# Six early experts placed in a written order among the last two token tiles of the attention, their output over their own rows, their adds behind ranked gathers

## The chip, the core and the metric

The kernel runs on one core of one Trainium2 chip. The metric is the device time of one launch in microseconds (us); three runs of the kernel before gave 1723.81, 1723.93 and 1724.05 us, a median of 1723.93 us.

## What is computed

Four layers run one after the other on a 4 x 512 x 512 input, in float32. Only the last two matter for the change: a cross attention over 1024 context rows, and a mixture of 32 experts of which every token uses eight.

```python
# cross attention (last but one layer)
scores = einsum('bsd,bmd->bsm', hidden_states, memory_tokens) * scale   # masked
attn = softmax(scores, axis=-1)
out = einsum('bsm,bmd->bsd', attn, memory_tokens)
...
# mixture of experts (last layer): TOP_K = 8 of NUM_EXPERTS = 32
routing_weights, selected = top_k(softmax(x2d @ gate_kernel), TOP_K)
routing_weights /= sum(routing_weights)
sorted_inputs = take(x2d, argsort(selected) // TOP_K)
w0 = ragged_dot(sorted_inputs, gate_proj, group_sizes)    # 512 -> 192
w1 = ragged_dot(sorted_inputs, up_proj, group_sizes)      # 512 -> 192
expert_out = ragged_dot(silu(w0) * w1, down_proj, group_sizes)   # 192 -> 512
output = einsum('BKE,BK->BE', unsorted(expert_out), routing_weights)
...
x = x + _L1_xattn_ref(_layernorm(x), ctx_2048, mask)
x = x + _L1_ffn_ref(_layernorm(x), gate_kernel, gate_proj, up_proj, down_proj)
```

## The kernel before

The 2048 tokens stand in 16 tiles of 128 (0 to 15). The scores of the attention (L972) run from 725.5 us of the profile; the two layers before them are not touched.

**Attention.** A software pipeline runs over the tiles: at step t tile t is normalised (`norm_q`), tile t-1 gets its scores (`scores`), tile t-2 reads the context (`readout`), tile t-3 picks its eight experts (`choose`), and tile t-4 is entered into the lists (`place_rows`). `readout` transposes the probabilities, multiplies with the context (16 passes on PE, L999), adds to the residual, stores that to the output (L1007) and normalises the result into a row buffer `xr`. `choose` transposes `xr`, multiplies with the router (L1018), takes the top eight (`sel`), and stores the row with its weights to DRAM (`xn_d`, for tiles 0 to 10 also `xa_d`). `place_rows` makes positions with two tiny products on PE (L1049, L1050) and writes the token numbers into the lists `il_d` with eight indirect scatters on POOL (L1062) per tile.

**Early experts.** After tile 10 is placed, the first 256 list entries of experts 0 to 5 are final (`start_early`). Such an expert is worked on with two row tiles gathered from `xa_d` (`early_rows`: two indirect gathers on POOL, L899, into one of four big buffers) while the lists of the rest are still being written. Experts 4 and 5 use the buffers of 0 and 1 again.

**Ranked experts.** When all tiles are placed, `cnt` holds the count of every expert. VectorE ranks the experts by count (eight or so operations on 128 x 1024 elements, L1154 to L1163); rank r then gets the fixed shape `FIXED[r]` (the first is 7 tiles of 126 rows). The place of a ranked expert's list is read into a register on SP, the list is loaded (`load_list`, L911), which waits for all scatters, its rows are gathered on POOL (`load_rows`, L899, one gather per tile), its weights come over SP (`fetch`: three transfers, L891 to L893, 768, 256 and 128 KB, into one of three buffers).

**One expert.** Rows are transposed (`turn`, L1192, copied from PSUM by ACT and DVE in turn, L1184 and L1182), multiplied with gate and up (`gate_up`, L1211, three products, with silu on ACT, L1216 and L1221, and products on DVE, L1218 and L1226), multiplied with down (L1235, L1238), scaled by the routing weight (`finish`, ACT L1247 and DVE L1245) into one of three tiles `y`, and added to the output with one indirect accumulating transfer on POOL per row tile (`add_rows`, L1254). The adds of an expert wait until the adds of the expert before have landed. In the loop the transposes of the next part stand between `gate_up` and `down` of this one.

**What sets the order.** In this stage no order is written: a scheduler places the instructions of each engine by its own estimates, keeping dependencies. `tc.issue_after(ins)` keeps what is inside behind `ins` on its queue. Each engine and each queue runs in order. The early experts were six members of the list `work`, ahead of the ranked ones, all in one loop, and so their place among the last tiles of the attention was the scheduler's.

Of the kernel before, what the change touches and what calls it, by code (L numbers as in the profile page):

```python
# [18 lines left out]
P = 128  # L19
# [4 lines left out]
EARLY = 6  # L24
# [24 lines left out]
def kernel(  # L49
# [829 lines left out]
    xrs = [route_p.tile([P, XW], F32, name=f"xr{i}") for i in range(4)]  # L879
# [39 lines left out]
    scatters, begun = [], []  # L919
    with tc.tile_pool(name="ctx2", bufs=1) as ctx2, tc.tile_pool(  # L920
        name="aw", bufs=2
    ) as aw, tc.tile_pool(name="aps_s", bufs=2, space=PSUM) as aps_s, tc.tile_pool(
        name="aps_t", bufs=2, space=PSUM
    ) as aps_t, tc.tile_pool(name="aps_o", bufs=2, space=PSUM) as aps_o:
# [40 lines left out]
        def scores(t):  # L965
            b = t // TPB
            qt = aw.tile([P, DC, P], F32, tag="qt", name="qt")
            transpose_to(aps_t, xns.pop(t), qt)
            ps = aps_s.tile([P, M], F32, tag="sc", name="sc")
# [19 lines left out]
        def readout(t):  # L989
# [3 lines left out]
            for h in range(2):  # L993
                transpose_to(
                    aps_t, s[:, bass.ts(h, M // 2)], pt[:, bass.ts(h, MC // 2), :]
                )
            ps = aps_o.tile([P, 512], F32, tag="o", name="o")
            for c in range(MC):
                nc.tensor.matmul(  # L999
                    ps[:, :D], pt[:, c, :], values[b][c // (MC // 2)][:, c % (MC // 2), :],  # L1000
                    start=(c == 0), stop=(c == MC - 1),
                )
# [8 lines left out]
        def choose(t):  # L1011
# [3 lines left out]
            transpose_to(aps_t, xr[:, :D], rt)  # L1015
            ps = aps_o.tile([P, 512], F32, tag="o", name="o")
# [27 lines left out]
        def place_rows(t):  # L1044
# [3 lines left out]
            ps = aps_o.tile([P, 512], F32, tag="o", name="o")  # L1048
# [26 lines left out]
        def start_early():  # L1075

            nonlocal run
            ps = aps_o.tile([P, 512], F32, tag="o", name="o")
# [16 lines left out]
        def early_rows(e):  # L1095
            i = (2, 0, 1, 3)[e % 4]
            pool = big3 if i == 3 else big
            xg = pool.tile([P, ER, XW], F32, tag=f"big{i}", name=f"big{i}")
            for c in range(ER):
                gather(xg[:, c, :], xa_d, early[e][1][:, c : c + 1], CUT * P + P)  # L1100
            early_xg[e] = xg

        load_ctx(0)
        for step in range(NTT + 4):
            if step < NTT and step % TPB == 1 and step // TPB + 1 < B:
                load_ctx(step // TPB + 1)
            if step < NTT:
                norm_q(step)
            if 1 <= step < NTT + 1:
                scores(step - 1)  # L1110
            if 2 <= step < NTT + 2:
                readout(step - 2)
            if 3 <= step < NTT + 3:
                choose(step - 3)
# [4 lines left out]
            if step - 4 == CUT:  # L1119
                with tc.issue_after(scatters[-1]):  # L1120
                    for e in range(4):
                        early_rows(e)
        ps = aps_o.tile([P, 512], F32, tag="o", name="o")
        nc.tensor.matmul(ps[:, :E], ones, run, start=True, stop=True)
        nc.vector.tensor_sub(cnt, ps[:, :E], base1)
# [3 lines left out]
    M2 = MI - P  # L1129
    TM = max(t for t, _ in FIXED)  # L1130
    with tc.tile_pool(name="er", bufs=3, reuse_waits="tile") as er, tc.tile_pool(
        name="ei", bufs=2, reuse_waits="tile"
    ) as ei, tc.tile_pool(
        name="eps_g", bufs=2, space=PSUM, reuse_waits="tile"
    ) as eps_g, tc.tile_pool(
        name="eps_t", bufs=2, space=PSUM, reuse_waits="tile"
    ) as eps_t, tc.tile_pool(
        name="eps_d", bufs=4, space=PSUM, reuse_waits="tile"
    ) as eps_d, tc.tile_pool(name="rw", bufs=1, reuse_waits="tile") as rw:
# [9 lines left out]
        key = rw.tile([P, E], F32, name="key")  # L1149
# [3 lines left out]
        sq = rw.tile(square, F32, name="sq")  # L1153
        nc.vector.tensor_tensor(sq, inner(key), outer(key), ALU.is_gt)  # L1154
        rank = rw.tile([P, E], F32, name="rank")
# [4 lines left out]
        def by_rank(name, v, dtype=F32, scale=1.0, shift=0.0):  # L1160
            nc.vector.tensor_mul(sq, hot, inner(v))
            f = rw.tile([P, E], F32, name=f"{name}_f")
# [17 lines left out]
        def copy(i, dst, ps):  # L1180
            if i % 2:
                nc.vector.tensor_copy(dst, ps)  # L1182
            else:
                nc.scalar.copy(dst, ps)  # L1184

        def turn(xg, t0, nt, q):

            xgt = ei.tile([P, DC, 512], F32, tag="xgt", name="xgt")
            for c in range(DC):
                ps = eps_t.tile([P, 512], F32, tag="tr", name="tr")  # L1190
# [9 lines left out]
        def gate_up(gu, xgt, nt, q):  # L1200


            n = nt * q
            h1 = ei.tile([P, 512], F32, tag="h1", name="h1")
            h2 = ei.tile([P, 512], F32, tag="h2", name="h2")
            sg = ei.tile([P, 512], F32, tag="sg", name="sg")
            ps = []
            for k in range(3):
                p = eps_g.tile([P, 512], F32, tag="g", name="g")
# [5 lines left out]
                if k == 0:  # L1215
                    nc.scalar.activation(sg[:, :n], p[:, :n], AF.Silu)  # L1216
                elif k == 1:
                    mul = nc.vector.tensor_mul(h1[:, :n], p[:, :n], sg[:, :n]).ins  # L1218
                else:
                    s2 = ei.tile([P, 512], F32, tag="s2", name="s2")  # L1220
                    nc.scalar.activation(s2[M2:, :n], p[:M2, :n], AF.Silu)  # L1221
                    for o in range(min(2, nt)):
                        def odd(v):
                            return v.rearrange("p (t q) -> p t q", q=q)[:, o::2, :]
                        half = LOW if o else UP
                        nc.vector.tensor_mul(  # L1226
# [342 lines left out]
```

## Time and profile before

| what | value |
|---|---|
| three runs | 1723.81, 1723.93, 1724.05 us |
| the profiled execution itself | 1739.66 us |
| its span, first to last instruction | 1737.9 us |
| mean clock granted to TensorE | 0.983 |
| PE, DVE, ACT, POOL busy | 95%, 44%, 29%, 34% of the span |
| last scores of the attention end | 989.5 us |
| first product of a ranked expert (128 x 378) | 1114.13 us |

Line numbers (L1211) are those of the kernel before. PE is the matmul engine and PEld its weight load, DVE VectorE, ACT ScalarE, POOL GpSimd, SPq the queue on which most transfers are issued. A float32 matmul shows as two instructions (two passes). "issue" as a reason for idle time means that the profile shows nothing that the engine waited for.

### The profile page before, as it was taken

What the parts mean: (1) busy time and instruction counts of PE and PEld (TensorE: products, weight loads), DVE (VectorE), ACT (ScalarE), POOL (GpSimd) and SP (SyncE); (2) the same over time, 40 slices, a digit from 0 to 9 for tenths busy, and PEclk for the clock granted to TensorE, in tenths of its full rate; (3) what the DMA queues carried; (4) which work ended last, traced back from release to release, by engine and by line L of the source; (5) the groups of instructions that cost most, each with busy time, mean ns of one, the idle gap of its engine ahead of it and who ended that gap; (6) DMA issues with size and microseconds to landing.
All of it is one profiled execution on the core that took longest, in us unless ns stands there. A gap on an engine that the chain in (4) does not pass through costs nothing.

```text
span 1737.9 us, 17749 instructions
## 1 busy us (share of the span) xinstructions
PE 1659.3 (95%) x6050; PEld 1010.7 (58%) x6050; DVE 763.0 (44%) x1715; ACT 506.9 (29%) x852; POOL 596.4 (34%) x522
## 2 busy tenths in 40 slices
PE   7998999999999999999999968899999999999996
PEld 2685657776777776545555445455555666544443
DVE  4683457755775554434444334222222223232322
ACT  2510333322331111146656431122222222222221
POOL 1000130101010100104434467555565666456654
PEclk9999999999999999999999979999999999999998
DMA  9313110000000000454331128867777887668774
GB/s 346 122 50 120 49 64 26 1 1 0 1 1 25 0 1 1 157 181 100 92 93 52 30 79 174 205 135 157 159 153 156 205 184 160 148 167 188 180 158 64
DMA packets 92717, 181.76 MB, mean 105 GB/s; under 512 B 23905, under 2 KB 24545, under 8 KB 92624
## 3 DMA queue, kind: packets, MB, share of 16 engines
q0 software_dynamic: 40560, 73.04, 22.4%
q1 hardware_dynamic: 51198, 106.72, 19.7%
q8 instruction: 48, 0.79, 0.2%
q10 hardware_dynamic: 866, 0.85, 0.2%
q14 instruction: 45, 0.37, 0.1%
HBM read 132.38 MB, written 51.62 MB: 106 GB/s over the span
## 4 chain that ended last, share of the span: by engine, by line
PE 82%; DMA 5%; issue 5%; DVE 4%; POOL 2%; ACT 2%; another core or an unknown queue 1%; ACTq 0%; POOLq 0%; DVEq 0%; SPq 0%
PE g L1211 18%; PE q L717 17%; PE dn L364 11%; PE dn L1235 6%; PE o L999 5%; PE sc L972 5%; PE gu L342 5%; PE dn L1238 4%; PE tr L1192 3%; DMA out_dram<-y,ids 2%; PE tr L167 1%; DMA x_sb<-in_cn_dram 1%; PE o L1018 1%; DMA big<-xa_d,near 1%; POOL out_dram L1254 1%
## 5 line engine op out<-in xcount | busy, mean ns | idle before, releaser
L1211 PE MATMUL g<-xgt,gu 128*128 128x256 f32 (+25 forms) x1248 | 384.2, 464 | 3.4 <-ACT sg L1216 2.0
L1211 PEld LDWEIGHTS g<-xgt,gu 128*128 128x128 f32 x1248 | 234.3, 192 | 164.5 <-issue 81.7
L1254 POOL DMA_INDIRECT out_dram<-y,ids x153 | 242.8, 1587 | 131.2 <-ACT y L1247 45.6
L899 POOL DMA_INDIRECT xg<-xn_d,ids x141 | 151.0, 1071 | 143.9 <-issue 125.9
L364 PE MATMUL dn<-wdn,h 128*128 128x512 f32 x448 | 200.3, 593 | 0.0
L1062 POOL DMA_INDIRECT il_d<-tok,slots x128 | 127.0, 992 | 193.2 <-DVE sel L1032 85.8
L717 PE MATMUL q<-big,s 128*128 128x256 f32 x768 | 173.6, 379 | 0.0
L717 PEld LDWEIGHTS q<-big,s 128*128 128x128 f32 x768 | 145.9, 190 | 19.8
L1235 PE MATMUL dn<-d,h 128*126 128x512 f32 (+8 forms) x306 | 150.4, 598 | 0.4 <-issue 0.4
L364 PEld LDWEIGHTS dn<-wdn,h 128*128 128x128 f32 x448 | 84.1, 190 | 92.8 <-issue 91.6
L717 PE MATMUL q<-big,wgu 128*128 128x256 f32 x576 | 132.4, 379 | 0.0
L1218 DVE TENSOR_TENSOR h<-g,sg 128x256 f32<-128x256 f32 (+25 forms) x52 | 27.0, 520 | 232.1 <-PE g L1211 197.3
L717 PEld LDWEIGHTS q<-big,wgu 128*128 128x128 f32 x576 | 109.3, 190 | 25.7 <-issue 9.3
L342 PE MATMUL gu<-big,wgu 128*128 128x256 f32 x512 | 116.5, 384 | 3.3 <-ACT sg L349 3.3
L999 PE MATMUL o<-big,pt 128*128 128x512 f32 x256 | 115.2, 602 | 4.1 <-issue 3.5
L972 PE MATMUL sc<-big,qt 128*128 128x512 f32 x256 | 114.4, 600 | 0.3 <-ACT qt L170 0.3
L342 PEld LDWEIGHTS gu<-big,wgu 128*128 128x128 f32 x512 | 97.7, 192 | 26.4 <-issue 8.5
L374 POOL TENSOR_TENSOR x_sb<-x_sb,y 128x512 f32<-128x512 f32 x16 | 19.8, 1270 | 258.3 <-DVE y L373 258.3
L278 POOL TENSOR_TENSOR x_sb<-x_sb,beta_t 128x512 f32<-128x512 f32 x16 | 23.7, 1509 | 235.2 <-ACT y L267 222.8
L1247 ACT ACTIVATE y<-dn,w 126x512 f32<-126x512 f32 (+8 forms) x82 | 56.3, 687 | 139.6 <-PE dn L1238 137.1
L731 ACT ACTIVATE sg<-q,wsu_t 128x256 f32<-128x256 f32 x96 | 45.4, 473 | 171.5 <-DVE q L753 84.0
L1192 PEld LDWEIGHTS tr<-ident,xg 126*128 126x128 f32 (+8 forms) x564 | 64.4, 141 | 53.1 <-ACT xgt L1184 20.2
(233 smaller groups left out, 1883.2 us busy)
## 6 DMA issues: line engine op xcount, KB each, us to landing
gu<-in_w_gu_dram SPq DMA_DIRECT2D x38, 768.0 KB
big<-in_cn_dram SPq DMA_DIRECT2D x10, 1024.0 KB
d<-in_w_dn_dram SPq DMA_DIRECT2D x38, 256.0 KB
big<-in_ct_dram SPq DMA_DIRECT2D x8, 1024.0 KB
x_sb<-in_cn_dram SPq DMA_DIRECT2D x12, 512.0 KB
d<-in_w_dn_dram SPq DMA_DIRECT2D x38, 128.0 KB
xn_d<-xr SPq DMA_DIRECT2D x16, 272.0 KB
x_sb<-in_x_dram SPq DMA_DIRECT2D x4, 1024.0 KB
```

The lines of the kernel that those rows point to most:

```text
L342: nc.tensor.matmul(ps[:, :n], wt[:, c, fs], xhs[b][:, c, cols], start=(c == 0), stop=(c == DC - 1),)
L364: nc.tensor.matmul(ps[:, :D], h[:, i * P : (i + 1) * P], wdn[:, fc, :], start=(fc == 0), stop=(fc == FC - 1),)
L717: nc.tensor.matmul(q[:, m * HS : (m + 1) * HS], w[:, m, k, :], x[:, k, :], start=(k == 0), stop=(k == 1),)
L899: ins = nc.gpsimd.indirect_dma_start(out=xg, out_offset=None, in_=src[:, :], in_offset=bass.IndirectOffsetOnAxis(ap=idx, axis=0), bounds_c ...
L972: nc.tensor.matmul(ps[:, bass.ts(h, M // 2)], qt[:, c, :], keys[b][h][:, c, :], start=(c == 0), stop=(c == DC - 1),)
L999: nc.tensor.matmul(ps[:, :D], pt[:, c, :], values[b][c // (MC // 2)][:, c % (MC // 2), :], start=(c == 0), stop=(c == MC - 1),)
L1062: ins = nc.gpsimd.indirect_dma_start(out=il_d[:, :], out_offset=bass.IndirectOffsetOnAxis(ap=slots[:, j : j + 1], axis=0), in_=tok[:, t : ...
L1192: nc.tensor.transpose(ps[:, h * q : (h + 1) * q], xg[:q, t0 + h, c * P : (c + 1) * P], ident[:q, :q],)
L1211: nc.tensor.matmul(p[:, :n], gu[:, c, k * P : (k + 1) * P], xgt[:, c, :n], start=(c == 0), stop=(c == DC - 1),)
L1235: nc.tensor.matmul(p[:q, :D], h1[:, bass.ts(i, q)], d1, start=True, stop=False)
L1238: nc.tensor.matmul(p[:q, :D], h2[half, bass.ts(i, q)], d2[half, :], start=False, stop=True)
L1254: ins = nc.gpsimd.indirect_dma_start(out=of[:, :], out_offset=bass.IndirectOffsetOnAxis(ap=idx, axis=0), in_=y, in_offset=None, bounds_che ...
```

## The change

The early experts leave the list `work` and its class `Early` goes. They get three functions: `T(e)` transposes in four steps (a generator), `G(e, fill)` is gate and up, taking one step of `fill` behind every third matmul, `D_(e)` is down, scaling, and the fetch of the weights of expert e+3. The result of `D_` is written over the gathered rows themselves. `readout` and `choose` become generators that stop once after their transposes; `readout` can take a step of `T` ahead of every second matmul. The order on PE, DVE and ACT from tile 14's readout to the last early expert is then the written one (`manual_schedule`); POOL and SP keep theirs.

```diff
-        def readout(t):
+        def readout(t, among=lambda: None):
...
+            yield
...
             for c in range(MC):
+                if c % 2:
+                    among()
...
         def early_rows(e):
-            i = (2, 0, 1, 3)[e % 4]
-            pool = big3 if i == 3 else big
-            xg = pool.tile([P, ER, XW], F32, tag=f"big{i}", name=f"big{i}")
+            if e < 4:
+                i = (2, 0, 1, 3)[e]
+                pool = big3 if i == 3 else big
+                xg = pool.tile([P, ER, XW], F32, tag=f"big{i}", name=f"big{i}")
+            else:
+                xg = ee.tile([P, ER, XW], F32, tag="xg", name="xg")
...
-                    for e in range(4):
+                    for e in range(3):
                         early_rows(e)
+        wts = {e: fetch(e) for e in range(3)}
...
+        def T(e):
+            xgt = xgts[e] = ee.tile([P, DC, ER * P], F32, tag="xgt", name="xgt")
+            for c in range(DC):
+                ps = ps_t.tile([P, 512], F32, tag="tr", name="tr")
+                for h in range(ER):
+                    nc.tensor.transpose(
+                        ps[:, h * P : (h + 1) * P],
+                        early_xg[e][:, h, c * P : (c + 1) * P], ident,
+                    )
+                copy(c, xgt[:, c, :], ps[:, : ER * P])
+                yield
+        def G(e, fill=iter(())):
...
+                for c in range(DC):
+                    nc.tensor.matmul(
+                        p[:, : ER * P], wts[e][0][:, c, k * P : (k + 1) * P], xgt[:, c, :],
+                        start=(c == 0), stop=(c == DC - 1),
+                    )
+                    if (k * DC + c) % 3 == 2:
+                        next(fill, None)
...
+        def D_(e):
+            xg = early_xg[e]
+            _, d1, d2 = wts.pop(e)
+            for i, p in enumerate(down(*hs.pop(e), ER, P, d1, d2)):
+                finish(i, p[:, :D], xg[:, i, :D], xg[:, i, D + e : D + e + 1])
+            if e + 3 < EARLY:
+                wts[e + 3] = fetch(e + 3)
+        last = NTT - 1
+        scores(last)
...
+        with tc.manual_schedule(engines=order):
+            turned = T(0)
+            r14, c13 = readout(last - 1, lambda: next(turned, None)), choose(last - 2)
+            next(r14)
+            next(c13)
+            whole(r14)
+            whole(c13)
+            place_rows(last - 3)
+            with tc.issue_after(scatters[-1]):
+                early_rows(3)
+            turned = T(1)
+            r15, c14 = readout(last, lambda: next(turned, None)), choose(last - 1)
+            next(r15)
+            next(c14)
+            whole(c14)
+            whole(r15)
+            place_rows(last - 2)
+            with tc.issue_after(scatters[-1]):
+                early_rows(4)
+            G(0)
+            c15 = choose(last)
+            next(c15)
+            D_(0)
+            whole(c15)
+            place_rows(last - 1)
+            with tc.issue_after(scatters[-1]):
+                early_rows(5)
+            turned = T(2)
+            G(1, turned)
+            place_rows(last)
...
+        with tc.manual_schedule(engines=order):
+            early_adds(0, scatters[-1])
+            for k in range(3):
+                work[k].load_list()
+            turned = T(3)
+            G(2, turned)
+            D_(1)
+            for k in range(3):
+                work[k].load_rows()
+                if k == 0:
+                    early_adds(1, gathers[-1])
+            for k in range(3, LISTS):
+                work[k].load_list()
+            turned = T(4)
+            G(3, turned)
+            D_(2)
+            work[0].load_weights()
+            early_adds(2, gathers[-1])
+            turned = T(5)
+            G(4, turned)
+            D_(3)
+            work[1].load_weights()
+            early_adds(3, gathers[-1])
+            G(5)
+            D_(4)
+            early_adds(4, gathers[-1])
...
+        xgt = turned(*parts[0])
+        D_(5)
+        early_p.close()
+        early_adds(5, gathers[-1])
```

Smaller parts: the scratch of the ranking lies in the row buffers `xr`, now one tile; the 32 one-column fills of `most` move from the end of the expert stage to its preparation; PSUM pools of the attention (`ps_t`, `ps_o`) live on into the expert stage, `ps_g` and `ps_d` take the banks of the scores, and the down products rotate over two banks of `ps_d` and two of `ps_o` instead of four of one pool. The ranked loop itself is the old one, without the early experts.

## The prediction

> **What bounds the kernel now.** I first read the page's busy shares and the row of granted clock: PE is busy 95% of the span, and its clock is below full in one stretch. I then cut the span into windows to find it.
>
> ```profile
> PE 1659.3 (95%) x6050; PEld 1010.7 (58%) x6050; DVE 763.0 (44%) x1715; ACT 506.9 (29%) x852; POOL 596.4 (34%) x522
> 985.00:998.00 13.00, 12.71 (x39) 6.09 (x38) 3.17 (x6) 2.74 (x5) 9.96 (x11) 1.00 0.27 27
> 998.00:1014.00 16.00, 8.73 (x31) 5.86 (x30) 3.62 (x19) 5.63 (x8) 7.78 (x8) 0.68 0.50 170
> 1014.00:1030.00 16.00, 11.13 (x49) 8.12 (x48) 4.70 (x31) 5.63 (x9) 10.07 (x11) 0.76 0.12 35
> 1030.00:1064.00 34.00, 27.31 (x87) 16.43 (x87) 18.86 (x39) 5.35 (x11) 26.09 (x55) 0.81 0.42 47
> 1064.00:1085.00 21.00, 19.75 (x87) 13.45 (x86) 6.82 (x15) 5.07 (x11) 13.60 (x12) 1.00 1.03 281
> 1085.00:1114.00 29.00, 21.42 (x81) 12.66 (x79) 5.57 (x13) 3.90 (x9) 19.05 (x17) 0.89 1.01 275
> 1114.00:1174.00 60.00, 59.69 (x203) 31.13 (x202) 17.02 (x32) 13.78 (x25) 30.73 (x23) 1.00 0.64 122
> ```
>
> A window's columns are: stretch, length, busy time of PE, PEld, DVE, ACT and POOL, granted clock, DMA share, GB/s. From 985 to 1114 us, the end of the attention and the six early experts, PE is busy 101 of 129 us: 28 us idle. The clock takes more: 0.68, 0.76, 0.81 and 0.89 mean that about 37 us ran at half; some 5 of them were idle, so 32 us of work took twice its time: 16 us. Idle and clock make 44 us. From the other side: attention's rest (scores 4.5, two readouts 14.3, transposes, routers and placements about 12, from their rows) and six experts at 9.34 us (G to G, 1063.99 to 1073.33), 56, need about 87 us of 129. So 41 to 44 us is the most that any order can return. After 1114 PE is full to 1720 us, and nothing there is touched.
>
> The chain of waits names what halted PE:
>
> ```profile
> 993.85 6.43 DMA big<-xa_d,near
> 1001.63 4.84 issue
> 1010.15 4.50 PE o L999 x8
> 1023.37 1.13 PE tr L167 x4
> 1025.21 1.92 PE o L1018 x8
> 1040.66 3.95 another core or an unknown queue x2
> 1053.17 4.33 another core or an unknown queue
> 1081.26 9.43 DMA big<-xa_d,near
> ```
>
> Gathered rows that land late (6.43 and 9.43 us after issue); the last tile's normalisation, for which nothing else was placed (PE empty 1020.2 to 1023.4); and halts with no visible releaser (at 1001.6, 1042, 1056, 1091 and 1105.6 us: 4.8, 3.5, 2, 1.1 and 2.9 us, together 14). Behind three halts the clock is at half: 1002 to 1012, 1023 to 1036.5, 1108 to 1114 us.
>
> **The change, step by step.** I follow PE through the built program's order, with durations from the rows, in the profile's own microseconds. Tile 15's scores and eight transposes end as before at 990.6.
>
> 1. Readout 14. The first of its eight matmul pairs ends at 991.5. The next instructions are now T(0)'s two transposes of expert 0's gathered rows. Those gathers stay on POOL behind the scatters of tile 11, so they still issue from 993.85; in the trace the transposes that wait for them ran at 1000.65 and 1001.30. Before, PE did the readout meanwhile; now all of it waits behind T(0): 9.8 us lost, to 1001.3.
>
> ```profile
> 993.85 1.05 POOL L899 DMA_INDIRECT big<-xa_d,near  x1 [0.30 <-issue]
> 1000.65 0.30 PE L1192 MATMUL tr<-ident,big 128*128 128x128 f32 x1 [2.07 <-DMA big<-xa_d,near]
> 1001.30 0.33 PE L1192 MATMUL tr<-ident,big 128*128 128x128 f32 x1 [0.35 <-issue]
> ```
>
> Then 14/16 of 7.13 and T(0)'s 4 x 0.44: 8.0. The clock has gone. After the idle stretch from 1001.6 to 1006.5 the row shows half speed until 1012, 5.5 us of work, so I add 2.75: end 1012.1. The Trainium skill ("TensorE: Matmul & The Clock Gate", "What's actually happening") says that the clock halves after about 3.4 us of idleness and returns after about 3.4 us of sustained work, which speaks against a stall in mid-readout. By that rule the addition would be an estimated 1.7 us instead of 2.75, and the forecast 1 us lower.
>
> 2. Router 13 (1.08), placing tile 12 (0.8), transposes of tile 15's probabilities (1.06): 1015.0. Transposing tile 14's row needs its normalisation. Behind readout 15 that took 3.8 us without the exp between (add 1018.78 to about 1022.5), so 1015.9: wait 0.9. Router 14 needs ACT to load exp (1.28), do one exp (0.32), two copies of tile 15's probabilities (1.07) and the row's copy (0.58): 1019.2, wait 2.7. Two waits with almost no matmul between them: I add 2 for the clock. Router 1.08, readout 15 with T(1) 8.9: 1032. Placing tile 13 included.
>
> 3. G(0) 5.45 and the row transposes 0.6 cover the 3.8 us of normalisation 15 that left PE empty before; D(0) 2.8 covers the copy for router 15 (1.08); placing 14 0.8: 1042.8. G(1) with T(2) 7.2, placing 15 and the count 1.2: 1051.2. G(2) began at 1063.99 before.
>
> 4. Left until the first ranked product: four rounds of 9.34, one D more (2.8), 0.9 for the larger transposes: 41.1. That makes 1092.3. DVE's ranking (operations of 1.2 us) now stands between early copies: 1 us.
>
> The rows of rank 0 decide whether that holds. Placing tile 12 is queued on DVE behind weights that wait for ACT's exp 13, after tile 14's normalisation: its scatters start at 1019, not 1010.28. POOL needs 10.2 us per tile (8 x 1.275) and 2.6 for two gathers, now three times between the scatters: tile 15's end at 1070.8, where before they ended at 1055.8. Landing 4.5 and list 2.0 ("974.00 4.51 DMA il_d<-tok,slots" and the list behind it) overlap the adds of expert 0 (2 x 1.9): rank 0's gathers from 1077.5, the third issued by 1081.6. With 6.43 to 9.43 us to land that is 1088 to 1091, and T(rank 0) is due at about 1087. I take 2 us of wait: first ranked product at 1095.3.
>
> ```profile
> 1081.26 1.08 POOL L899 DMA_INDIRECT big<-xa_d,near  x1 [0.30 <-issue]
> 1090.82 0.30 PE L1192 MATMUL tr<-ident,big 128*128 128x128 f32 x1 [1.42 <-DMA big<-xa_d,near]
> 1116.03 1.54 POOL L1254 DMA_INDIRECT out_dram<-y,ids  x1 [7.10 <-DMA out_dram<-y,ids]
> 1132.19 1.62 POOL L1254 DMA_INDIRECT out_dram<-y,ids  x1 [2.06 <-DMA out_dram<-y,ids]
> ```
>
> 5. The halts without a releaser: bounds 0 and 23 us (14 and the half clock behind them, 9). Three of the five stand beside a DMA share near 1, where the new order still works; but the order gives PE more to do between waits. I take 5, one such halt: 1100.3 against 1114.1, a gain of 14.
>
> 6. Edits at nothing: the fills of `most` (1.1 us of POOL) stand early, under the feed forward's matmuls; scratch in `xr` moves nothing; the PSUM banks for down stay four; weights 0 to 2 were already fetched long before. Weights 3 to 5 issue as buffers come free. On SP expert 5's down weights and rank 0's weights queue behind the five lists, so they issue near 1077, and are due at 1088 and 1095: 10 us of cover, and at some 280 GB/s (row 1064 to 1085) 1.5 MB takes 5.4 us.
>
> The sum: -14 on this execution's 1739.66 gives 1725.7. It lies 15.7 us above the median, and I can't see where. Spread evenly, a gain of 0.8% makes 1723.93 into **1710 us**.
>
> **Rivals.** *Adds back up (slower).* Adds of experts 2 to 5 stand on POOL behind rank 2's gathers with no gather between them, so each waits until the last has landed. Gathers of ranks 0 to 2 are 19 x 1.37 and the adds of expert 1 3.9: adds 2 start at 1107.4. With landings of 4.7 (the row at 1132.19: the add before ended at 1127.45) and 3.9 per pair, rank 3's two gathers (2.7) and one more landing, rank 0's adds begin at 1141.7, and the first of the three `y` tiles is free at about 1152. PE needs it for the fourth part at 1100.3 + 57.7 = 1158. With landings as slow as the gather's 9.43, five times 4.7 us more, it is free at 1175.5: PE stalls 17.5, a loss of 3.5 after the gain: 1739.66 + 3.5, in the median 1727. It decides from landings of about 6 us and loses from about 9. For it: 7.10 in the row at 1116.03. Against it: DMA share falls to 0.64 after 1114. With every halt of point 5 back the result is similar: 1095.3 + 23 is 1118, 1728. Together 0.24.
>
> *The halts are the profile's own (no change).* If the 15.7 us between profile and median lie in this stretch, the unprofiled kernel loses only about 28 there, and the new order's own waits (9.8 + 2.75 + 3.6 + 2 + 3) take 21 of a possible 28 at most: gain 3 to 7, some 1721. For it: halts of this kind stand nowhere else in the trace. Chance 0.14.
>
> *A better order than I think.* No halts, rows on time: 1092, a gain of 22: 1702. Chance 0.15. That the order is not the written one is excluded by the built program: PE shows it.
>
> **Numbers.** Forecast (1705 to 1720) 0.47, better 0.15, no change 0.14, slower 0.24. The likeliest is 1710. The range 1698 to 1728 takes in both bounds of point 5 and the adds. About 0.2% (3.4 us) is what a measurement can tell from no change: faster 0.62, same 0.14, slower 0.24.
>
> **What would show it.** PE idle some 9 us at 991.5 in readout 14, with T(0) waiting for the DMA, and a half clock behind it; no gap between readout 15 and router 15; last scatter near 1071; first 128 x 378 product near 1095 to 1100; a wait for `y` in rank 1's second part only if adds back up. I am wrong if the gather lands before 991, if the halts all return, or if the first ranked product gains and the end does not.

## The result, and the profile after

The changed kernel is slower, by a third of a percent: 1730.16 us (1728.25 to 1732.34, 7 runs) beside 1723.93 us (1722.21 to 1727.35, 7 runs) for the kernel before; ratio 1.0033, 95% interval 1.0021 to 1.0045. The forecast was 1710.

The two profiled executions say the opposite: 1739.66 us before, 1730.79 after, 8.9 us less. The profiled execution after is one of its own timed runs; the one before is none of its own, and stood 15.7 us above their median. The same 8.9 us stand at the first ranked product, 1114.13 before and 1105.19 after; from there to the end both take 623.8 us. So what differs lies ahead of that product, nearly all of it behind 985 us. The windows of the changed kernel over the stretches that were shown for the kernel before (same columns):

```profile
985.00:998.00 13.00, 8.83 (x26) 3.89 (x24) 3.37 (x8) 3.67 (x7) 9.86 (x10) 0.89 0.29 27
998.00:1014.00 16.00, 12.10 (x42) 6.79 (x42) 2.51 (x6) 2.32 (x4) 2.99 (x3) 0.70 0.32 112
1014.00:1030.00 16.00, 12.19 (x39) 6.67 (x38) 4.71 (x28) 6.32 (x10) 8.88 (x9) 0.79 0.12 40
1030.00:1064.00 34.00, 32.84 (x162) 24.76 (x161) 22.63 (x59) 12.14 (x22) 21.25 (x20) 1.00 0.90 137
1064.00:1085.00 21.00, 18.20 (x69) 11.96 (x68) 7.95 (x22) 3.64 (x8) 12.03 (x11) 0.92 0.62 61
1085.00:1114.00 29.00, 19.70 (x68) 11.18 (x68) 5.96 (x13) 4.05 (x8) 19.48 (x18) 0.82 0.93 262
```

PE is busy for 104 of the 129 us, against 101 before. The idle time has moved: the middle (1030 to 1064) is nearly full and at full clock now, where it was 27 of 34 us at 0.81; the ends carry the idleness. The waits of PE in this stretch (total, number, longest) name all 25 us of it, and none is without a releaser (an event in the profile that ended the wait):

```profile
PE tr L1350 <- DMA xg<-xn_d,ids: 9.3, 3, 4.4
PE tr L1208 <- DMA big<-xa_d,near: 7.7, 2, 7.5
PE tr L167 <- ACT pt L170: 3.4, 2, 3.1
PE tr L1208 <- DMA xg<-xa_d,near: 2.8, 2, 1.6
PE g L1228 <- ACT sg L1171: 1.2, 1, 1.2
PE o L1038 <- ACT rt L170: 0.7, 1, 0.7
```

Line numbers in a run's rows are those of its own kernel; here L1350 are the transposes of ranked rows, L1208 those of early rows. So 9.3 us go to rank 0's rows, 7.7 to expert 0's in the middle of readout 14. The timeline of PE, POOL and SP's queue shows both, and the links between them:

```profile
1001.64 0.45 PE L1208 MATMUL tr<-ident,big 128*128 128x128 f32 x1 [7.52 <-DMA big<-xa_d,near]
1018.43 1.01 POOL L1082 DMA_INDIRECT il_d<-tok,slots  x1 [16.68 <-DVE slots L1079]
1074.65 0.97 POOL L1082 DMA_INDIRECT il_d<-tok,slots  x1 [0.30 <-issue]
1081.83 4.30 SPq L916 DMA_DIRECT2D ids<-il_d  x5
1086.32 1.13 POOL L904 DMA_INDIRECT xg<-xn_d,ids  x1 [6.92 <-DMA ids<-il_d]
1091.31 0.33 PE L1350 MATMUL tr<-ident,xg 126*128 126x126 f32 x1 [2.05 <-DMA xg<-xn_d,ids]
1096.03 0.47 PE L1350 MATMUL tr<-ident,xg 126*128 126x126 f32 x1 [4.39 <-DMA xg<-xn_d,ids]
1105.19 7.89 PE L1369 MATMUL g<-xgt,gu 128*128 128x378 f32 x24
```

Read from the bottom up: the first ranked product at 1105.19 waits for rows that POOL gathers from 1086.32; the gather waits for a list, loaded from 1081.83; the lists wait until the last scatter, issued at 1074.65, has landed; and the first scatter of tile 12 could not start before 1018.43, because POOL waited 16.7 us for its slots. From the last scatter to the first ranked product it is 30.5 us.

### The profile page after: what moved, and what is told of

Its sections match the earlier page's. It is cut to its first block, busy times and chain, and to the rows that moved or that the text cites. A ratio compares the mean times of both kernels' runs of the same rounds, so it can differ in the third digit from the quotient of the medians.

```text
span 1729.0 us, 17724 instructions
## 1 busy us (share of the span) xinstructions
PE 1653.6 (96%) x6050; PEld 1008.9 (58%) x6050; DVE 764.8 (44%) x1715; ACT 508.5 (29%) x853; POOL 596.8 (35%) x522
## 4 chain that ended last, share of the span: by engine, by line
PE 82%; DMA 6%; DVE 5%; ACT 3%; issue 2%; POOL 1%; SPq 0%; ACTq 0%; POOLq 0%; DVEq 0%
PE g L1369 19%; PE q L717 17%; PE dn L364 11%; PE o L1018 6%; PE dn L1186 6%; PE sc L988 5%; PE gu L342 5%; PE dn L1189 4%; DMA il_d<-tok,slots 2%; PE tr L1350 2%; DMA out_dram<-y,ids 2%; PE tr L167 1%; DMA x_sb<-in_cn_dram 1%; DVE h L1179 1%; PE o L1038 1%
## 5 line engine op out<-in xcount | busy, mean ns | idle before, releaser
L1369 PE MATMUL g<-xgt,gu 128*128 128x360 f32 (+24 forms) x1104 | 346.0, 470 | 0.0
L1369 PEld LDWEIGHTS g<-xgt,gu 128*128 128x128 f32 x1104 | 205.0, 190 | 149.9 <-issue 76.7
L1383 POOL DMA_INDIRECT out_dram<-y,ids x141 | 224.5, 1592 | 110.9 <-ACT y L1198 34.4
L1018 PE MATMUL o<-big,pt 128*128 128x512 f32 x256 | 119.4, 615 | 3.8 <-ACT pt L170 3.8
L1350 PEld LDWEIGHTS tr<-ident,xg 126*128 126x128 f32 (+8 forms) x564 | 65.0, 142 | 60.3 <-ACT xgt L1164 20.3
```

What stands on the lines that cost most here:

```text
L1018: nc.tensor.matmul(ps[:, :D], pt[:, c, :], values[b][c // (MC // 2)][:, c % (MC // 2), :], start=(c == 0), stop=(c == MC - 1),)
L1350: nc.tensor.transpose(ps[:, h * q : (h + 1) * q], xg[:q, t0 + h, c * P : (c + 1) * P], ident[:q, :q],)
L1369: nc.tensor.matmul(p[:, :n], gu[:, c, k * P : (k + 1) * P], xgt[:, c, :n], start=(c == 0), stop=(c == DC - 1),)
L1383: ins = nc.gpsimd.indirect_dma_start(out=of[:, :], out_offset=bass.IndirectOffsetOnAxis(ap=idx, axis=0), in_=y, in_offset=None, bounds_che ...
```

## The experiments

Each set below ran on one chip with the kernel before beside it as a yardstick (time: median, lowest and highest of its runs). The sets differ in that yardstick, which turned out to be the main finding. The record names the chips of sets 1 to 6 as 1, 5, 3, 2, 15 and 2; sets 4 and 6 have the same number and 13 us between them.

| set | kernel before, us | what ran |
|---|---|---|
| first measurement | 1723.93 (1722.21 to 1727.35) | changed 1730.16 |
| 1 | 1751.01 (1737.04 to 1757.57) | b_again, t0_in_r15, place_early, both |
| 2 | 1747.91 (1732.18 to 1755.60) | after_again, t0_again, a_plain, a_nowts |
| 3 | 1750.90 (1736.85 to 1757.29) | b_plain, six_first, t0_six, after_third |
| 4 | 1734.77 (1730.32 to 1745.06) | b_side, t0_one, b_third |
| 5 | 1724.25 (1721.69 to 1728.40) | after_fourth, six_again |
| 6 | 1747.44 (1736.40 to 1756.58) | t0_six_again |

### Set 1: undo T(0) in readout 14, place tiles earlier

`b_again` is the kernel before, unchanged.

> The kernel before, unchanged, profiled a second time. Theory H (the five halts without a releaser belong to that one profiled execution and not to the timed runs): this profile shows none or other ones, and its first ranked product (128 x 378) comes near 1098 us instead of 1114.13, its span near 1722. Rival (the halts are in every run of the kernel): the same halts near 1002, 1042, 1056 and 1106 us, first ranked product near 1114, while the time stays near 1724 and the 15.7 us lie elsewhere.

`t0_in_r15` moves expert 0's transposes one readout later:

```diff
-            turned = T(0)
-            r14, c13 = readout(last - 1, lambda: next(turned, None)), choose(last - 2)
+            r14, c13 = readout(last - 1), choose(last - 2)
...
-            turned = T(1)
+            turned = T(0)
...
-            G(0)
+            G(0, T(1))
```

> The changed kernel with one edit: T(0) is taken among readout 15 instead of readout 14, T(1) inside G(0). Theory A (the wait for expert 0's rows inside readout 14, 1001.6 us, holds up PE and, through tile 12 to 15's placing, the rows of rank 0): readout 14 ends near 1000, everything behind it some 11 to 13 us earlier, first ranked product near 1093 instead of 1105.2, time near 1717. Theory B (rank 0's rows are late for reasons behind that: scatters that wait for landings and lists, whatever PE does): first ranked product no earlier than 1102, time 1727 or more.

`place_early` moves `place_rows(last - 3)`, with the early rows behind it, ahead of readout 14, and the later tiles' placements forward likewise; `both` is the two edits together.

> The changed kernel with one edit: each tile is placed as soon as its choice is known (12 ahead of readout 14, 13 ahead of router 14, 14 behind readout 15, 15 at the first step among G(1)), with the gathers of experts 3 to 5 behind them; T(0) stays in readout 14. Theory B (the row chain sets the first ranked product): last scatter issued near 1055 instead of 1075.6, rank 0's rows there before PE wants them, first ranked product at PE's own 1095, time near 1720. Theory A (only PE's wait in readout 14 counts): within 2 us of 1730.

> Both edits together. A and B both: PE's own path is 11 to 13 us shorter and the rows come in time: first ranked product near 1084, time near 1709. If the adds of experts 2 to 5 then back up on POOL (three tiles y full in the fourth part), PE waits for y near 1140 to 1150 and the time stays at 1714 or above.

Measured: b_again 1744.26; t0_in_r15 1727.31 (ratio to the kernel before 0.9886, 0.9842 to 0.9930); place_early 1741.11 (0.9967, 0.9937 to 0.9997); both 1745.63 (0.9986, 0.9960 to 1.0012). The yardstick itself was 27 us above its first measurement, so none of this could be compared with 1730, and the sizes expected are not confirmed. What can be read: the profile of b_again has halts without a releaser again (3.7, 7.3 and 2.0 us are the longest) and its first ranked product at 1118.98, so theory H falls in its wording: they do not belong to one execution. t0_in_r15 lies where theory B put it (first ranked product 1102.35, 1727 us). In place_early tile 12's scatters did start at 1002.88 instead of 1018.43, and the wait of the ranked transposes shrank to 0.5 us. But the last scatter was issued only at 1077.18, and the first ranked product stood at 1112.28, because PE now lost some 12 us more, 8 of them where nothing visible held it. In `both`, DVE takes the result of readout 14 more than 16 us after its last matmul (the first row runs to 1000.06):

```profile
993.03 7.03 PE L1018 MATMUL o<-big,pt 128*128 128x512 f32 x16
1016.30 0.75 DVE L1023 SCALAR_TENSOR_TENSOR x_sb<-o,rinv,x_sb 128x512 f32<-128x512 f32 x1 [17.58 <-remote]
```

I call that a late result from here on: the record of the matmul has ended, the reader waits for nothing else, and starts microseconds later. In the profiles it stands as "issue", "remote" or "another core or an unknown queue". The profile gives the ends of matmuls by a model, so the name says when the reader starts, not what held the result.

### Set 2: the changed kernel on the same chip, without gathers, without loads

> The changed kernel itself, beside the one before on the same chip. In this set of runs the kernel before needs about 1751 us (1737 to 1758) where the first measurement had 1724, and its profile here (1744 us) loses PE time to halts whose releaser is not shown (TensorE's results reach DVE and ACT up to 9 us after the records of the matmuls). Theory H (those halts belong to the conditions of the run, and the written order has them too): after is also some 15 to 25 us slower here than its first 1730, so 1742 to 1755, ratio to before 0.996 to 1.004. Theory R (the halts belong to the old order): after stays at 1728 to 1733 with no such halt, ratio 0.985 to 0.990, and the sign of the comparison depends on where it is run.

> Expert 0's transposes stand in readout 15 instead of readout 14, nothing else is changed. It gave 1727 (1717 to 1731) before. Theory W (what the changed kernel loses is its own wait in readout 14, 7.5 us, with the half clock behind it): faster than the changed kernel of the same set by 5 to 12 us. Rival N (the rows of rank 0 set the end in either, and halts hit both alike): within 3 us of it.

In `a_plain` the early experts work on rows that stand together instead of their own:

```diff
-                gather(xg[:, c, :], xa_d, early[e][1][:, c : c + 1], CUT * P + P)
+                nc.sync.dma_start(out=xg[:, c, :], in_=xa_d[c * P : (c + 1) * P, :])
```

> The changed kernel with the early experts' rows loaded by plain transfers of SyncE (128 rows that stand together, so the early experts compute on other rows) in place of the twelve gathers of POOL; all else stands as it is. Theory G (POOL's gathers between the scatters are what costs: T(0)'s wait of 7.5 us, three pairs of 2.6 us on POOL ahead of the last scatters, and the halts without a releaser): no wait over 2 us at T(0), the last scatter issued by about 1068 instead of 1075.6, rank 0's gathers from 1078, the first product of 128x378 at 1090 to 1096, and no halts: about 1712 to 1720. Theory S (the scatters, or the chip, cause them): PE still halts for over 5 us in all between 1000 and 1080 without a transfer that it waits for, first ranked product at 1100 or later.

`a_nowts`: `wts[e + 3] = fetch(e + 3)` becomes `wts[e + 3] = held`, the weights of expert e, so experts 3 to 5 compute with those of 0 to 2.

> The changed kernel with experts 3, 4 and 5 computed with the weights of 0, 1 and 2, so that their three loads (1.15 MB each, in flight between 1040 and 1090) are not made. Theory C (these loads share the DMA engines with the scatters and with the lists, and so make rank 0's rows late): scatters of tile 15 land in 3.5 to 5 us instead of 7 to 10.65, rank 0's gathers start 4 to 6 us sooner, the wait of the ranked transposes falls from 9.3 us to 0 to 4, first ranked product 4 to 8 us sooner than in the changed kernel. Theory Q (POOL's own queue makes them late, not the DMA engines): landings at most 1 us shorter, that wait still 8 us or more, time within 2 us of the changed kernel's.

Measured: after_again 1735.05 (1731.65 to 1746.92; ratio 0.9945, 0.9917 to 0.9973). So here the change wins. The time moved by 5 us from its first 1730, the yardstick's by 24: nearer to theory R than to H, though its trace is not free of late results, as R wanted (copies of ACT and DVE at 1047.3 start over 3 us late). t0_again 1731.14 (1723.92 to 1740.45), 4 us less than the changed kernel in the medians, which the scatter of the runs does not separate from none: a late result of 4.9 us at readout 14 took the place of the wait that was removed. Nor did its rows of rank 0 gain. Its last scatter stood 10.2 us sooner than in after_again (1065.53 against 1075.71), its first ranked product 1.6 us sooner. The list has to wait for the ranking on DVE as well, whose last result that it needs, `start`, came only at 1077.61, behind a late result of PE that held DVE for 7.3 us:

```profile
1077.61 0.17 DVE L1330 TENSOR_SCALAR start<-xr 128x32 int32<-128x32 f32 x1
1079.12 4.45 SPq L916 DMA_DIRECT2D ids<-il_d  x5
```

a_nowts 1735.56: theory C falls. The last scatter at 1075.35 is followed by the lists at 1082.05, 6.7 us later, where it is 6.9 in after_again, and the medians are 0.5 us apart: these loads are not what makes the lists late. The wait of 8 us or more that Q named is not there either; late results at 1047 to 1061 (up to 12 us of idle DVE) brought PE there later than the rows.

a_plain: 1715.94 (1714.02 to 1718.75), with no late result between 985 and 1114. Its PE waits (a fifth is 0.3 us):

```profile
PE tr L1350 <- DMA xg<-xn_d,ids: 10.9, 3, 4.8
PE tr L167 <- ACT pt L170: 3.1, 1, 3.1
PE g L1228 <- ACT sg L1171: 2.5, 2, 1.4
PE o L1038 <- ACT rt L170: 0.7, 1, 0.7
```

Theory G holds, as a bundle: the run does not part the waits for gathered rows, the gathers' time on POOL and the late results. And the first line is a second lesson: rank 0's rows are as late relative to PE as ever (10.9 us), though everything stands 13 us earlier. The last scatter is at 1060.05, the first ranked product at 1092.55, 32.5 us behind it.

### Set 3: the kernel before without gathers, and all gathers ahead

`b_plain` is the edit of a_plain in the kernel before; `six_first` lets the six `early_rows` stand together behind tile 11's scatters; `t0_six` adds the edit of t0_in_r15:

```diff
                 with tc.issue_after(scatters[-1]):
-                    for e in range(3):
+                    for e in range(6):
                         early_rows(e)
...
-            with tc.issue_after(scatters[-1]):
-                early_rows(3)
```

(the same for 4 and 5)

> The kernel before with the early experts' rows loaded by plain transfers of SyncE in place of POOL's twelve gathers (the early experts compute on other rows); the order on TensorE is the same. Theory G (in these runs TensorE's late results come only where gathers run): no result of TensorE reaches DVE or ACT over 1 us late before 1060, first product of 128x378 at 1085 to 1095 instead of 1114 to 1119, about 1712 to 1722; the median of the changed kernel with plain loads was 1716, so without gathers the two orders differ by less than 5 us. Theory S (scatters back to back, or the old order itself): late results between 1035 and 1060 as before, 1735 or more.

> The changed kernel with all six early experts' gathers together, behind tile 11's scatters, where POOL stood idle from 1002 to 1018 us; none is left between the scatters of tiles 12 to 15. Theory K (the chain last scatter, list, rank 0's gather, first ranked product, some 31 us long, sets the end of this stretch): last scatter issued 5 to 8 us sooner, at about 1067 to 1070, first product of 128x378 at 1098 to 1101, 4 to 8 us less than the changed kernel. Rival P (TensorE's path sets it): first ranked product within 2 us of the changed kernel's, the ranked transposes' wait of 9 to 11 us gone without gain. Rival B (a burst of twelve gathers makes TensorE's results late): a halt of 6 us or more at readout 14, slower than the changed kernel.

> As six_first, with expert 0's transposes in readout 15 too. Theory K: both savings add up, last scatter at 1056 to 1060, first ranked product at 1090 to 1095, 10 to 16 us less than the changed kernel (about 1718 to 1724). Rival B: the burst of twelve gathers (to about 1011 us) holds the result of readout 14 until 1 to 2 us behind its end, so DVE takes it at 1011 to 1013 instead of 1003 to 1005, tile 12's scatters start at 1017 or later, and the gain over the changed kernel is under 6 us.

> The changed kernel again, as the yardstick of this set, since sets run on different chips: 1730 to 1737. If the chip of this set gives the kernel before about 1724, as the first measurement did, the changed kernel should be slower than it here (ratio 1.002 to 1.005); if it gives 1740 to 1751, faster (ratio 0.990 to 0.997).

Measured: b_plain 1722.91 (1722.68 to 1725.48). Without gathers the kernel before is at its first 1724 in a set where it needs 1751 with them. The orders differ by 7 us without gathers (1716 to 1723, in two sets; under 5 was expected), in favour of the change. Theory G's numbers for the profile were only partly met: the first ranked product stood at 1097.81, not at 1085 to 1095, and one late result (the router's product of tile 15, recorded until 1018.7 and taken at 1026.17) remained, so gathers are not the only occasion.

six_first 1728.31 (1726.15 to 1729.71), after_third 1734.88 (ratio 0.9925, 0.9888 to 0.9963): 6.6 us less, theory K, though the last scatter (1071.44) and the first ranked product (1103.21) stood 1.4 and 2.2 us behind the bounds given. t0_six 1728.80, no better: rival B. Its DVE and POOL:

```profile
1010.62 1.00 POOL L904 DMA_INDIRECT xg<-xa_d,near  x1 [0.30 <-issue]
1013.69 0.75 DVE L1023 SCALAR_TENSOR_TENSOR x_sb<-o,rinv,x_sb 128x512 f32<-128x512 f32 x1 [15.52 <-remote]
```

The first line is the twelfth gather, the second DVE taking readout 14, whose last matmul is recorded up to 1002.1: 11.6 us late, 2 us behind the end of the burst of gathers. PE waits 11.6 us for it at L1069.

### Set 4: gathers that nobody waits for

`b_side` keeps b_plain's plain loads and adds the gathers again, into a tile that nothing reads (its early experts, too, work on rows that are not theirs):

```diff
+                aside = side.tile([P, XW], F32, tag="aside", name="aside")
+                gather(aside, xa_d, early[e][1][:, c : c + 1], CUT * P + P)
```

`t0_one` is t0_again with experts 1 and 2 gathered behind tile 12's scatters.

> The kernel before with plain loads for the early experts' rows, as b_plain (1723), and POOL's twelve gathers made all the same, into tiles that nothing reads. Theory E (the gathers themselves, by what they do on the chip, make TensorE's results late): late results of 2 us and more between 995 and 1060 come back, time 1735 to 1750, though nothing waits for a gathered row. Rival D (TensorE waits for the gathered rows in a way that its records do not show): no late results, 1721 to 1727.

> As t0_again (expert 0's transposes in readout 15), with only expert 0's two gathers behind tile 11's scatters; those of experts 1 and 2 follow tile 12's scatters. In four profiles the result of readout 14 reached DVE 0.4 to 2.1 us behind the end of POOL's burst (1002.8 to 1005.0, 1001.3 to 1002.8, 1011.6 to 1013.7, 1015.9 to 1016.3). Theory E: with the burst ended at about 997.5, DVE takes it at 999 to 1000.5, when readout 14 itself ends, tile 12's scatters start 3 to 5 us sooner (1005 to 1007 instead of 1009 to 1011.5), about 1723 to 1728. Rival N (the lateness belongs to that place of the program, not to the burst): DVE takes it at 1003 or later again.

> A profile of the kernel before on the chip of this set: 1735 to 1757, with TensorE's results 1.5 to 9 us late between 1000 and 1060, first product of 128x378 at 1112 to 1122. If it stands near 1724 instead, this chip is like that of the first measurement, and b_side must be read against it.

Measured: b_side 1735.22 (1727.25 to 1740.35; ratio to the kernel before 0.9993, 0.9967 to 1.0017): as slow as the kernel before in that set, and 12 us above b_plain in the other. No transfer of gathered rows can hold PE in it, and yet its timeline has:

```profile
1004.77 0.61 PE L1051 MATMUL o<-run,ones 128*128 128x32 f32 x2
1005.20 1.09 PE L167 MATMUL tr<-ident,s 128*128 128x128 f32 x4
1009.03 1.00 POOL L900 DMA_INDIRECT aside<-xa_d,near  x1 [0.30 <-issue]
1012.73 0.19 DVE L1023 COPY lg<-o 128x32 f32<-128x32 f32 x1 [11.92 <-remote]
1013.06 3.75 PE L1000 MATMUL o<-big,pt 128*128 128x512 f32 x4 [6.77 <-DVE mv L147]
```

DVE waits 11.9 us for a router product that stands on PE's record before 1004.8, and gets it 2.7 us behind the end of the last of the twelve gathers (the third row); PE waits 6.8 us in turn. Later it has results that are 9.1 and 11.7 us late, at 1053 and 1057, 43 and 47 us behind that gather, while POOL issued scatters. Theory E has what it asked for: late results without anyone waiting for a gathered row. That the gathers make them is not shown by it: b_plain did not run in this set, so the 12 us are a comparison across sets, and two of the late results are far from any gather.

t0_one did what E asked at that place: DVE took readout 14 at 998.67, tile 12's scatters started at 1005.19 (expected 1005 to 1007). But PE halted 8.4 us at 1038, behind expert 4's gathers (1033.63 to 1036.01), and the time was 1732.90 (0.9980, 0.9959 to 1.0001), not 1723 to 1728. Here, with the gathers moved, the late result moved too. b_third, a single run of the kernel before: 1731.41, the first ranked product at 1107.00; better than expected, as was the whole set. It still shows the halts:

```profile
1005.65 1.92 PE L1018 MATMUL o<-router_t,rt 128*128 128x32 f32 x8 [3.97 <-issue]
1050.78 0.69 PE L1192 MATMUL tr<-ident,big 128*128 128x128 f32 x2 [8.52 <-issue]
```

### Sets 5 and 6: the conditions of the first measurement again

> The changed kernel in one more set, on whatever chip it gets. So far the pairs before/changed were 1724/1730 (first measurement), 1748/1735 and 1751/1735: the changed kernel hardly moves while the kernel before moves by 27 us. If that is so, the changed kernel gives 1729 to 1736 here too, and the ratio follows from the kernel before alone: about 1.003 where that needs 1724, 1.000 where it needs 1733, 0.992 where it needs 1748.

> six_first again beside the changed kernel. Theory K (the chain from the last scatter to the first ranked product): 4 to 8 us less than the changed kernel in this set as well, 1723 to 1730, the last scatter 3 us or more sooner. Rival: the gain of the first time (6.6 us) was the chip's, and here it is under 2 us.

> t0_six again, on whatever chip this set gets. On a chip where the kernel before needs about 1724, TensorE's results should not be late behind the burst of gathers; then the transposes' move from readout 14 to readout 15 should pay what it could not pay at t0_six: DVE takes readout 14's result at about 1000, tile 12's scatters start at 1006 to 1010, the last scatter stands at 1056 to 1064, first ranked product at 1090 to 1096, 1710 to 1717. Where the kernel before needs 1735 or more: late result at readout 14 as before, 1726 to 1731, no better than six_first.

Set 5 had a kernel before of 1724.25, as in the first measurement. after_fourth 1728.84 (ratio 1.0026, 1.0016 to 1.0035): the first result again, and its trace has no late result, gathers or not. six_again 1722.08 (1719.97 to 1724.31; ratio 0.9983, 0.9975 to 0.9992): faster than both. Its three longest PE waits, and then rows of two timelines: the last scatter and the first ranked product of after_fourth, and the last scatter, rank 0's first gather and the first ranked product of six_again:

```profile
PE tr L1208 <- DMA big<-xa_d,near: 8.7, 2, 8.4
PE tr L1344 <- DMA xg<-xn_d,ids: 7.8, 2, 4.0
PE tr L167 <- ACT pt L170: 3.4, 2, 3.1
```

```profile
1074.50 0.97 POOL L1082 DMA_INDIRECT il_d<-tok,slots  x1 [0.30 <-DMA il_d<-tok,slots]
1104.16 7.89 PE L1369 MATMUL g<-xgt,gu 128*128 128x378 f32 x24
```

```profile
1065.79 0.97 POOL L1082 DMA_INDIRECT il_d<-tok,slots  x1 [0.30 <-issue]
1076.73 1.14 POOL L904 DMA_INDIRECT xg<-xn_d,ids  x1 [6.19 <-DMA ids<-il_d]
1097.44 7.89 PE L1363 MATMUL g<-xgt,gu 128*128 128x378 f32 x24
```

The last scatter is 8.7 us sooner, the first ranked product 6.7, the median 6.8. The wait for rank 0's rows is no shorter (7.8 us, 5.7 in after_fourth). PE comes sooner, the rows come sooner.

In set 6 the kernel before needed 1747.44. t0_six_again 1728.66, as its expectation had it for that case, with a late result of 7.6 us at readout 14. What t0_six gives under the conditions of set 5 was not measured.

## Why the prediction was wrong

**Steps 1 to 3 held** (forecasts in brackets). Expert 0's rows in readout 14: 7.5 us of wait (9.8), because PE came there at 994.1 (991.5); readout 14 ends at 1011.9 (1012.1); the two waits before router 14 take 3.1 and 0.7 (0.9 and 2.7); G(2) begins at 1048.7 (1051.2). The clock behind the first wait, by windows of PE around it:

```profile
994.10:1001.60 7.50, 0.02 (x1) 0.00 (x0) 0.32 (x2) 1.24 (x2) 5.89 (x6) 0.71 0.66 94
1001.60:1005.00 3.40, 3.13 (x5) 1.47 (x6) 0.00 (x0) 0.37 (x1) 0.15 (x1) 0.50 0.72 284
1005.00:1008.40 3.40, 3.40 (x8) 1.64 (x7) 0.42 (x1) 0.00 (x0) 0.00 (x0) 0.63 0.02 5
```

Half clock lasted for the first 3.4 us of work and three quarters of the next 3.4 (0.63), some 5.9 us, which costs 2.95, and the 2.75 taken from the row was near it. The Trainium skill ("TensorE: Matmul & The Clock Gate", "What's actually happening") has the clock return after about 3.4 us of sustained work; the estimate of 1.7 us by that rule is too low here.

**Step 4, rank 0's rows: mis-sized.** The text took 2 us of wait, with the last scatter at 1070.8 and the first gather at 1077.5. (Its own terms, four tiles of 10.2 and three pairs of 2.6 from 1019, make 1067.6; where the other 3.2 come from it does not say.) Measured: last scatter 1075.6 (1074.65 and its own 0.97), lists from 1081.83, first gather 1086.32, and 9.3 us of wait. Of the 8.8 us by which the gather was late, 4.8 are the last scatter's, and 4 the two links behind it, priced from rows where they stood alone. The rest of PE's path was right: 1105.19 less 9.3, and less some 2 us for the clock behind those waits (0.50 from 1093 to 1103, over 4.2 us of work), is about 1093.8; the forecast without its wait was 1093.3.

I had treated the rows as a wait to be added; they are a chain that begins at the last scatter. In twelve of the fifteen profiles of the written order it is 29 to 33 us from the last scatter's issue to the first ranked product (30.5 in the first, 29.7 in after_fourth, 31.7 in six_again); in the three of the kernel before it is 53 to 66, and PE never waits for rank 0's rows there. The other three are place_early (35.1), where the lists came 13.9 us behind the last scatter, and `both` and t0_again (39.0 and 39.6), where the ranking on DVE, held by late results, let the lists go. So what stands ahead of the last scatter (the slots that wait for ACT's exp, three pairs of gathers) moves the end nearly one for one as long as the ranking is done sooner: 8.7 us gave 6.7 in six_again, 9.4 gave 8.6 in six_first, 15.7 gave 14.2 in a_plain, but 10.2 gave 1.6 in t0_again.

**Step 5 and the sum: wrong, and the larger error.** "It lies 15.7 us above the median, and I can't see where. Spread evenly": the 15.7 us were not spread. The halts without a releaser, which I left standing as 5 of 14 us, are late results. (By PE's own rows two of the five, at 1056 and 1105.6, wait for ACT, 2.0 and 2.9 us; it was ACT that started late.) They do not all stand beside gathers: around 1002 POOL gathers, at 1042 and 1056 it issues scatters. Whether they come differs between sets: the kernel before is up to 27 us slower in some sets than in others, the changed kernel up to 6. The timed runs of the first measurement stood at 1724, which is where b_plain stands without gathers. That there were no halts in them is inferred, since no profile of the kernel before under such conditions exists; after_fourth, under those conditions, has none. The first profile looks like one taken under the other conditions: every later profile is of one of the timed runs beside it, and this one is not. So most of what the forecast subtracted was not there to be removed. In numbers: of the 20 us between 1710 and 1730, 5 are the gain in the profile's own time (14 forecast, 8.9 found), and 15 come from carrying it over to a median that had never paid for it.

**The rivals.** "The halts are the profile's own" had, as far as is inferred above, the mechanism of the first measurement, at a chance of 0.14, and the wrong size: 1721, because it used the same 2 us for rank 0's rows (7.3 short) and nothing for the rows of experts 4 and 5 (2.8). With both it is 1731; that this comes so near 1730 is partly luck, since its 9.8 us in readout 14 were 2.3 too many. "Adds back up" did not happen: the adds of experts 2 to 5 began at 1119, 1127, 1138 and 1146, some 12 us later than forecast (1107.4 for expert 2), POOL waited 4.4 to 7.8 us for landings between them, and still PE never waited for `y`. "A better order than I think" did not come true; a_plain is 7 us below b_plain, across two sets, once the rows come at no cost.

**What remains open.** Why results of PE reach DVE and ACT late beside gathers, and why in some sets and not in others. Taking the gathers out took 28 and 19 us off within a set (b_plain, a_plain); late results come without anyone waiting for gathered data (b_side); and at readout 14 the end of the burst of gathers often, not always, marks the release (in t0_six_again DVE got its result 2.2 us ahead of the burst's end). Two things in the traces were not followed up. First, it is TensorE's signals that come late, not their readers: the semaphore update (the signal that a result is done) that DVE waits for in `both` is recorded at 1016.27, 0.03 us before DVE starts, and in after_again none is recorded between 1042.1 and 1047.1, though PE works on to 1044.8, and then six come within 0.25 us. Second, about a tenth of TensorE's semaphore updates are missing from every trace of sets 1 to 4 and 6, and from the first profile of the kernel before (1107 recorded of 1228); they are complete in the three traces taken where the kernel before needs 1724 (the changed kernel's first, after_fourth and six_again), and none of these three has a late result. So what differs between the sets may lie in how an execution was recorded as well as in the chip. No run parts the two.

## What to carry to other kernels

A profile that stands 1% above its own timed runs can hold something that those runs did not pay for, and idle time without a releaser is the first suspect: price a change once with it and once without it, and do not carry a gain over in proportion. Where scatters feed a list, a gather and then a product, follow that chain link by link, and ask what is queued ahead of its first link and what else its links wait for. Here moving three pairs of gathers out from between the scatters into 16 us in which POOL stood idle was worth 6.6 and 6.8 us in the two sets where it ran, and in the set like the first measurement it made the difference between slower and faster than before.

## What the runs showed of the hardware

- Results of TensorE reached DVE and ACT 2 to 12 us late in a kernel whose indirect gathers nobody reads (b_side), by the ends that the profile gives matmuls. With gathers that are read, after_fourth and six_again had no late result; without any, b_plain had one, of 7.5 us.
- The same kernel before took 1724, 1735, 1748 and 1751 us in different sets. Kernels without these gathers, run four times each, were steady within 5 us in sets where that one scattered by 20 (1722.68 to 1725.48 beside 1736.85 to 1757.29); but so was six_first, with them (1726.15 to 1729.71).
- From the issue of the last scatter (128 four-byte entries) to the list's load it took 6.1 us (six_again) to 12.5 us (t0_six_again) where the ranking was done in time; 6.7 in a_nowts without the weight loads, 6.9 in after_again with them.
